# The border of a graph layer and the order of the layer behind it: halved products, an adjacency widened by columns, and one written order

## The chip, the cores and the metric

The kernel runs on one core of a Trainium2 chip. The metric is the device time of one execution in microseconds (us), the median over runs. Five engines matter: TensorE (PE, matrix products and transposes), VectorE (DVE), ScalarE (ACT), GpSimd (POOL) and SyncE (SP, which starts the DMAs). Each of the first four works through its own queue of instructions in order; semaphores make one engine wait for another.

## The reference

Four graph layers run one after another on `x` of shape 16 x 1024 x 64 (batch, node, feature) with one 1024 x 1024 adjacency matrix; each ends in a residual and a normalization over the 64 features:

```python
x = _layernorm(x + _L0_gnn_ref(x, L0_gnn_W, L0_gnn_a, adj), axis=-1)
x = _layernorm(x + _L1_gnn_ref(x, L1_gnn_w0, L1_gnn_b0, L1_gnn_wa, L1_gnn_ba, adj), axis=-1)
x = _layernorm(x + _L2_gnn_ref(x, adj, L2_gnn_W, L2_gnn_a), axis=-1)
x = _layernorm(x + _L3_gnn_ref(x, adj, ...), axis=-1)
```

Layers 0 and 2 are attention with one score per node pair, layer 3 has four heads. Layer 1, which this case is about, has a softmax whose score depends on the neighbour alone, feature by feature:

```python
feat = softplus(x * (INV_SQRT2 * w0) + b0)
scores = feat * wa + ba
attn = softmax(where(adj > 0, scores, -1e9), over the neighbours)
out = einsum('bijd,bjd->bid', attn, feat)
```

So with `E = exp(scores)` layer 1 is `(adj @ (E * feat)) / (adj @ E)`: two products with the plain adjacency, then a quotient.

## The kernel before

The nodes lie in C = 8 chunks of P = 128, the batch in NG = 4 groups of 4 (`xg[g]`), each group in two halves q of two batches.

**Layer 0** (`gat_layer`, lines 900 to 1199) goes batch by batch, t = 0 to 15, with a slot for each of the 8 chunks; tasks of neighbouring batches (evicting, projecting, dividing, residual, statistics, storing) are placed in slots `(t, k)`. Its order is written out by hand: the loop stands under `tc.manual_schedule`, so every engine gets its instructions in program order. The parameter `own` says how many slots behind the last batch belong to that loop; what comes later is returned as the list `ending`.

**Layer 1, preparation** (`prep_l1`, from line 1709) makes, for a group g and half q, nine tasks: `size`, `decay`, `above`, `log` (ACT: the softplus in pieces, 128 x 1024 each), `feature` (DVE adds them), `turn` (PE: 8 transposes of f into the PSUM tile `pf`), `exponents` (DVE finds a maximum over `pf`, ACT makes the exponentials `t`), `back` (PE: 8 transposes of t into the PSUM tile `pe`; ACT rounds that to `hi`, DVE makes `f * pe` and the rest `lo = pe - hi`), and `weighted` (ACT rounds `f * pe` to `hi`, DVE makes its `lo`). So each value is carried as a pair hi + lo in the matmul's rounded type. Group 0 is prepared up to `exponents` within layer 0.

**Layer 1, products** (`product_l1`, line 1829): for each chunk `ic` of 128 nodes, 16 matmuls of 128 x 512 add up into one PSUM tile `po` of the pool `ps_a`, which has two buffers. The stationary operand is a 128 x 128 piece of `aR`, the adjacency in the rounded type; the moving operand holds both halves q, numerator and denominator. `aR` is made from the 16-bit `aT` by eight casts of 128 x 1024 (line 1858), one for each row chunk k, alternately on DVE and ACT, so a product needs all eight.

**Layer 1, quotient** (`average`, line 1840): ACT takes Ln and Exp of the denominators (reciprocal), DVE refines it and multiplies (lines 1846 to 1848, which read `po`), subtracts from x (line 1851) and takes statistics (line 1853, 4 times). At the end of a group `moments`, `root` and `shift` turn these into scale and shift, and `rows` applies them on ACT (line 780, 32 rows of 128 x 64 for a group, four calls of 8).

In layer 1 the loops are not under the hand-written order: the program states tasks in some order, and a planner of the compiler, which knows the engines and the dependencies, decides the order of each engine's queue. In the profile DVE's parts of `average` and of `prep_l1` stand interleaved instruction by instruction.

**The border.** Before the first product of layer 1 stand, in the queues: the eviction of layer 0's last batch (ACT, lines 1022 and 1026), its projection (PE, lines 1043 and 1047), the store of batch 13 (ACT, line 780), the eight casts, the two `back` and the two `weighted` of group 0.

PSUM has room for eight banks: `ps_t` 2, `ps_a` 2, and in layer 0 `ps_g` and `ps_u` with 2 each. In layer 1 `pf` and `pe` use a pool `ps_l` of two tiles of two banks, in the place of `ps_g` and `ps_u`. Layer 2's first steps (`l2_ahead`) run within the last group of layer 1.

Of the kernel before, what the change touches and what calls it, by code (L numbers as in the profile page):

```python
# [8 lines left out]
F32 = mybir.dt.float32  # L9
# [7 lines left out]
P = 128  # L17
# [565 lines left out]
def fast_path(  # L583
# [24 lines left out]
    nc = tc.nc  # L608
    B, N, D = x.shape
    C = N // P  # L610
# [3 lines left out]
    GB = 4  # L614
    NG = B // GB
# [1093 lines left out]
    def prep_l1(g, q):  # L1709
# [36 lines left out]

        def back():
            if q == 0:
                his[g] = l1["halves"].tile([P, C, 2, 2, P], F32R, tag="hi", name=f"hi{g}")
                los[g] = l1["halves"].tile([P, C, 2, 2, P], F32R, tag="lo", name=f"lo{g}")  # L1750
            t = h["t"]
            pe = l1["psum"]("pe")
            for c in range(C):
                nc.tensor.transpose(pe[:, c, :], t[:, c, :], ident)
            hi, lo = his[g][:, :, q, 1, :], los[g][:, :, q, 1, :]
            nc.scalar.copy(hi, pe)
            nc.vector.tensor_tensor(h["f"], h["f"], pe, ALU.mult)
            nc.vector.tensor_tensor(lo, pe, hi.bitcast(F32), ALU.subtract)
# [5 lines left out]

        return [size, decay, above, log, feature, turn, exponents, back, weighted]

# [3 lines left out]
    for task in gat_setup(w_0, "l0", False):  # L1770
        task()
    with tc.tile_pool(name="ps_g", bufs=1, space=bass.MemoryType.PSUM, reuse_waits="tile") as ps_g, tc.tile_pool(
        name="ps_u", bufs=2, space=bass.MemoryType.PSUM, reuse_waits="tile"
# [34 lines left out]
        for q, todo in enumerate(l1_tasks):  # L1808
            t = 7 + 2 * q
            places = (t, 0), (t, 2), (t, 4), (t, 6), (t + 2, 2), (t + 2, 7), (t + 3, 5)  # L1810
            for place, task in zip(places, todo):
                extra.setdefault(place, []).append(task)
        ahead, go = gat_layer(w_0, "l0", False, 5)
        first(ahead)
# [6 lines left out]
    ))  # L1821
    l1_psum = ExitStack()
    ps_l = l1_psum.enter_context(tc.tile_pool(name="ps_l", bufs=2, space=bass.MemoryType.PSUM, reuse_waits="tile"))
    with tc.tile_pool(name="l1", bufs=2, reuse_waits="tile") as pool:
        l1["halves"] = pool
        l1["psum"] = lambda name: ps_l.tile([P, C, P], F32, tag="l", name=name)
        aR = pool.tile([P, C, N], F32R, tag="aR", name="aR", bufs=1)

        def product_l1(g, ic):
            po = ps_a.tile([P, 2, 2, P], F32, tag="acc", name=f"po{g}_{ic}")  # L1830
            for k in range(C):
                for e in (his[g], los[g]):
                    nc.tensor.matmul(  # L1833
                        po.rearrange("p q k f -> p (q k f)"), aR[:, k, ic * P : (ic + 1) * P],
                        e[:, k].rearrange("p q k f -> p (q k f)"),
                        start=(k == 0 and e is his[g]), stop=(k == C - 1 and e is los[g]),
                    )
            return po

        def average(g, ic, po, st):  # L1840
# [13 lines left out]

        ending[0]()
        for i, task in enumerate([l1_tasks[q][-2 + i] for q in range(2) for i in range(2)]):
            for k in range(2 * i, 2 * i + 2):
                (nc.scalar.copy if k % 2 else nc.vector.tensor_copy)(aR[:, k, :], aT[:, k, :])
            task()
        last = ending[1:]  # L1860
        for g in range(NG):
            ahead = [[] for _ in range(C)]
            for q in range(2 if g + 1 < NG else 0):

                for ic, task in zip((q, q, q, q, q + 1, q + 2, q + 2, q + 4, q + 5), prep_l1(g + 1, q)):
                    ahead[ic].append(task)
            if g + 1 == NG:
                for ic, task in zip((1, 2, 3, 3, 4, 5, 6, 6), l2_ahead):
                    ahead[ic].append(task)
            st = pool.tile([P, C * GB, 6], F32, tag="st1", name=f"st{g}")  # L1870
            for ic in range(C):
                po = product_l1(g, ic)
                average(g, ic, po, st)
                for task in ahead[ic] + last[ic : ic + 1]:
                    task()
            y = xg[g].rearrange("p c b d -> p (c b) d")
            mo = {}

            root, finish = moments(st)

            def shift(mo=mo, end=finish):
                mo["n"] = end()

            def rows(c, y=y, mo=mo):
                scaled(y, y, mo["n"], range(c * 8, c * 8 + 8))

            last = [root, shift] + [lambda c=c, rows=rows: rows(c) for c in range(C * GB // 8)]
    l1_pools.close()
# [78 lines left out]
    with tc.tile_pool(name="ps_g", bufs=1, space=bass.MemoryType.PSUM, reuse_waits="tile") as ps_g, tc.tile_pool(  # L1967
        name="ps_p", bufs=1, space=bass.MemoryType.PSUM, reuse_waits="tile"
    ) as ps_p:
        places = [(15, j) for j in (0, 1, 2, 3, 4, 5, 6, 7)]  # L1970
        extra = {p: [task] for p, task in zip(places, ahead)}
        for p, task in zip(((0, 0), (0, 1), (0, 3), (0, 7), (1, 3), (1, 7)), last):
            extra.setdefault(p, []).append(task)

        ending = l2_go(extra)
# [130 lines left out]
```

## Time and profile before

| what | us |
|---|---|
| median of 3 runs | 1978.29 |
| lowest and highest run | 1972.04, 1978.98 |
| profiled execution, its own time | 1970.04 |
| its span, first to last instruction | 1967.8 |
| layer 0 with loading, to its last aggregating matmul | 0 to 279.4 |
| first and last product of layer 1 | 291.4 and 431.0 |
| layer 2's first aggregating matmul | 437.0 |

Over the span PE is busy 96%, DVE 90%, ACT 68%, POOL 4%; the granted PE clock is 0.984 on average. The busy time is an average over stages with different limits, so this document reads the stretch from 280 to 437 us by itself. A line of the timeline gives start, duration, engine, source line, operation, operands and count; in brackets stands the time that the engine sat idle before it and what released it.

### The profile page before, as it was taken

Reading aid. Unit: us, or ns where it says so; the run is one execution under the profiler, and the core shown is the slowest. Engines: PE = TensorE matmul, PEld = TensorE weight load, DVE = VectorE, ACT = ScalarE, POOL = GpSimd, SP = SyncE. Lnnn points to the kernel's source line nnn. Section 1 sums busy time; section 2 is a strip of 40 time slices with the busy share of each in tenths; the row PEclk is TensorE's granted clock in tenths of the full one; section 3 lists DMA queues with packets and bytes.
Section 4 is the critical chain, followed back from the end, with each engine's and each line's share of the span. In section 5 each row is a group of like instructions: output and inputs, shape, how many; then the busy total and the mean of one; then the engine's idle time right before and its main releaser. Section 6 shows DMA issues by size and latency. Waiting matters only on the chain.

```text
span 1967.8 us, 25841 instructions
## 1 busy us (share of the span) xinstructions
PE 1879.4 (96%) x9545; PEld 767.6 (39%) x9545; DVE 1762.7 (90%) x2963; ACT 1332.3 (68%) x2344; POOL 83.0 (4%) x77
## 2 busy tenths in 40 slices
PE   7999989989888899999999999999999999999985
PEld 4444437863333333333333333333333333333332
DVE  5899988879999777798999989999899898998997
ACT  5356567857667776667767767677666776776653
POOL 0000000000000000000000000000000000000001
PEclk8999999999999999999999999999999999999998
DMA  7000000000000120000000000000000100010000
GB/s 179 1 1 1 1 1 1 1 1 1 1 1 3 51 56 12 12 12 19 22 17 12 20 25 12 17 18 22 17 12 18 28 12 17 12 28 17 12 17 18
DMA packets 45748, 35.90 MB, mean 18 GB/s; under 512 B 37295, under 2 KB 37616, under 8 KB 45614
## 3 DMA queue, kind: packets, MB, share of 16 engines
q1 hardware_dynamic: 45310, 34.14, 6.7%
q8 instruction: 77, 1.26, 0.3%
q14 instruction: 57, 0.47, 0.1%
q10 hardware_dynamic: 304, 0.03, 0.0%
HBM read 29.45 MB, written 4.70 MB: 17 GB/s over the span
## 4 chain that ended last, share of the span: by engine, by line
PE 70%; DVE 22%; ACT 5%; issue 1%; DMA 1%; POOL 0%; SPq 0%; DVEq 0%; POOLq 0%; ACTq 0%
PE y L1351 19%; PE s L1336 19%; DVE e L991 7%; PE y_l L1003 6%; PE po L1833 5%; PE y L1516 4%; PE s L1491 4%; DVE e L1344 4%; PE u_l L1015 3%; DVE e L1509 2%; DVE junk L1501 1%; PE phT L1310 1%; ACT e L1340 1%; PE poT L1378 1%; PE ph2T L1452 1%
## 5 line engine op out<-in xcount | busy, mean ns | idle before, releaser
L1340 ACT ACTIVATE e<-s,shift 128x1024 f32<-128x1024 f32 x512 | 539.3, 1123 | 221.2 <-PE s L1336 221.2
L1344 DVE TENSOR_TENSOR e<-e,aT 128x1024 f32<-128x1024 f32 x512 | 596.4, 1215 | 12.9 <-ACT e L1340 12.9
L1336 PE MATMUL s<-hT 64*128 64x512 f32 x2048 | 491.6, 604 | 1.4 <-ACT hT L1319 0.9
L1351 PE MATMUL y<-e,vals 128*64 128x512 f32 x2048 | 485.6, 601 | 5.5 <-DVE e L1344 4.3
L991 DVE SCALAR_TENSOR_TENSOR e<-G_l,q,aT 128x1024 f32<-128x1024 f32 x256 | 315.4, 1275 | 6.4 <-ACT G_l L968 6.3
L1336 PEld LDWEIGHTS s<-hT 64*128 64x128 f32 x2048 | 183.5, 186 | 289.0 <-issue 149.6
L1003 PE MATMUL y_l<-e,vals_l 128*64 128x512 f32 x1024 | 254.2, 616 | 26.9 <-DVE e L991 20.1
L1351 PEld LDWEIGHTS y<-e,vals 128*64 128x64 f32 x2048 | 135.9, 137 | 273.5 <-issue 200.3
L1509 DVE TENSOR_TENSOR e<-e,aT 128x1024 f32<-128x1024 f32 x128 | 156.2, 1225 | 9.8 <-DVE junk L1501 0.5
L1501 DVE SCALAR_TENSOR_TENSOR junk<-e,aN 128x1024 bf16<-128x1024 f32 x120 | 146.1, 1218 | 0.0
L1496 ACT ACTIVATE e<-s,shift 128x1024 f32<-128x1024 f32 x128 | 138.4, 1114 | 0.4 <-PE s L1491 0.4
L1516 PE MATMUL y<-e,h2v 128*64 128x512 f32 x512 | 127.2, 599 | 0.9 <-DVE e L1509 0.9
L1491 PE MATMUL s<-h2T 64*128 64x512 f32 x512 | 125.8, 591 | 0.0
L1003 PEld LDWEIGHTS y_l<-e,vals_l 128*64 128x64 f32 x1024 | 62.3, 138 | 160.4 <-issue 75.7
L1833 PE MATMUL po<-hi,aR 128*128 128x512 f32 x256 | 102.7, 402 | 11.1 <-ACT hi L1762 7.3
L1279 POOL PARTITION_ALL_REDUCE gtop<-top x48 | 55.3, 1152 | 1268.7 <-DVE top L1277 970.0
L1833 PE MATMUL po<-lo,aR 128*128 128x512 f32 x256 | 101.0, 395 | 0.0
L780 ACT ACTIVATE x<-m,bn_shift,bn_rstd 128x64 f32<-128x64 f32 x256 | 88.5, 430 | 0.0
L1491 PEld LDWEIGHTS s<-h2T 64*128 64x128 f32 x512 | 50.0, 186 | 60.2 <-issue 37.3
L1383 ACT COPY zT<-poT 64x512 f32<-64x512 f32 x124 | 72.0, 581 | 1.3 <-PE poT L1378 0.2
L1516 PEld LDWEIGHTS y<-e,h2v 128*64 128x64 f32 x512 | 36.6, 138 | 76.4 <-issue 58.5
L978 ACT ACTIVATE vals_l<-x,p 128x64 f32<-128x64 f32 (+1 forms) x256 | 64.3, 339 | 0.0
(270 smaller groups left out, 1876.1 us busy)
## 6 DMA issues: line engine op xcount, KB each, us to landing
r<-inverse SPq DMA_DIRECT2D x62, 256.0 KB
adj<-in_adj_dram SPq DMA_DIRECT2D x16, 512.0 KB
x<-in_x_dram SPq DMA_DIRECT2D x16, 256.0 KB
out_dram<-res SPq DMA_DIRECT2D x15, 256.0 KB
rows<-yT SPq DMA_DIRECT2D x62, 4.0 KB
sums<-rows SPq DMA_DIRECT2D x31, 8.0 KB
inverse<-rt SPq DMA_DIRECT2D x31, 8.0 KB
out_dram<-res SPq DMA_DIRECT2D x2, 128.0 KB
```

Of the source, the lines that this page charges most:

```text
L991: nc.vector.scalar_tensor_tensor(e, G[b - b % 2][:, b % 2, :], pq[b - b % 2][1][:, k, b % 2 : b % 2 + 1], aT[:, k, :], ALU.max, ALU.mult,)
L1003: nc.tensor.matmul(held["y"][h * D : (h + 1) * D, :], vals[b][:, k, :], e[:, h * HALF : (h + 1) * HALF], start=(k == 0), stop=(k == C - 1),)
L1336: nc.tensor.matmul(s[:, i, :], hT[rows, k * P : (k + 1) * P], hT[rows, cols], start=True, stop=True)
L1340: nc.scalar.activation(e, s, AF.Exp, bias=shifts[b, n])
L1344: nc.vector.tensor_tensor(e, e, bc_mid(aT[:, k, h * HALF : (h + 1) * HALF], 2), ALU.mult)
L1351: nc.tensor.matmul(held[h][i * D : (i + 1) * D, :], vals[b][:, k, :], e[:, i, :], start=(k == 0), stop=(k == C - 1),)
L1491: nc.tensor.matmul(s[:, i, :], hT[rows, (i + k // CH) % 2, k % CH * P : (k % CH + 1) * P], hT[rows, 0, :], start=True, stop=True,)
L1496: nc.scalar.activation(e, s, AF.Exp, bias=shifts[b])
L1501: nc.vector.scalar_tensor_tensor(junk.rearrange("p c q -> p (c q)").bitcast(BF16), e.rearrange("p i q -> p (i q)"), 1.0, aN[:, k, :], ALU. ...
L1509: nc.vector.tensor_tensor(e, e, aT[:, k, :].rearrange("p (i q) -> p i q", i=2), ALU.mult)
L1516: nc.tensor.matmul(held["o"][h * D : (h + 1) * D, :], vals["out", b][:, k, :], e[:, h, :], start=(k == 0), stop=(k == C - 1),)
L1833: nc.tensor.matmul(po.rearrange("p q k f -> p (q k f)"), aR[:, k, ic * P : (ic + 1) * P], e[:, k].rearrange("p q k f -> p (q k f)"), start ...
```

## The change

Five edits, all in layer 1 and its two borders.

1. `back` is cut into `turn_back` (the 8 transposes) and `halves` (the ACT and DVE part). For half 0 of group 0 the transposes move into layer 0's last slots, `(15, 7)`. For this `ps_g` stays open through layer 1; `ps_l` has one tile, and the PSUM tiles of layer 1 come from the two pools in turn (`either`).
2. `aR` is widened by column pairs (`widen(i)`: 128 x 8 x 256, four casts in place of eight): only the first comes before the first product.
3. The first two chunks' products of group 0 are done in halves q: 64 matmuls of 256 columns in place of 32 of 512, all `hi` first, then all `lo`; half 1 is split up while half 0 is being multiplied.
4. `own` goes from 5 to 4: the store of batch 13 leaves the border and comes in chunk 2 of layer 1's first group. `rows` works in eight calls of 4 instead of four of 8.
5. The whole of layer 1 goes under `tc.manual_schedule`: the queues take the written order. In it `average` of a chunk stands behind the next chunk's product (`late`), and the preparation of the next group has its chunks: half 0 in 0,0,1,1,2,2,3,3,4,5 and half 1 in 2,2,3,3,4,4,5,5,6,7, in the order of the ten tasks.

```diff
@@ prep_l1
-        def back():
+        def turn_back():
+            h["pe"] = l1["psum"]("pe")
+            for c in range(C):
+                nc.tensor.transpose(h["pe"][:, c, :], h["t"][:, c, :], ident)
+
+        def halves():
...
-            t = h["t"]
-            pe = l1["psum"]("pe")
-            for c in range(C):
-                nc.tensor.transpose(pe[:, c, :], t[:, c, :], ident)
+            pe = h["pe"]
@@ layer 0
+        extra.setdefault((B - 1, 7), []).append(l1_tasks[0][7])
-        ahead, go = gat_layer(w_0, "l0", False, 5)
+        ahead, go = gat_layer(w_0, "l0", False, 4)
@@ layer 1
+        def product_l1(g, ic, po=None, q=None):
+            po = po or ps_a.tile([P, 2, 2, P], F32, tag="acc", name=f"po{g}_{ic}")
+            part = slice(0, 2) if q is None else slice(q, q + 1)
+            order = [(k, e) for k in range(C) for e in (his[g], los[g])]
+            if q is not None:
+                order = [(k, e) for e in (his[g], los[g]) for k in range(C)]
...
+        def widen(i, copy):
+            cols = slice(i * 2 * P, (i + 1) * 2 * P)
+            copy(aR[:, :, cols], aT[:, :, cols])
...
-        ending[0]()
-        for i, task in enumerate([l1_tasks[q][-2 + i] for q in range(2) for i in range(2)]):
-            for k in range(2 * i, 2 * i + 2):
-                (nc.scalar.copy if k % 2 else nc.vector.tensor_copy)(aR[:, k, :], aT[:, k, :])
-            task()
-        last = ending[1:]
+        stored, projected, *last = ending
+        last.insert(2, stored)
+        def opening():
+            (pe_0, halves_0, weighted_0), (pe_1, halves_1, weighted_1) = (l1_tasks[q][7:] for q in range(2))
+            projected()
+            widen(0, nc.vector.tensor_copy)
+            pe_1()
+            halves_0()
+            weighted_0()
+            pos = [product_l1(0, ic, q=0) for ic in range(2)]
+            halves_1()
+            weighted_1()
+            for ic, po in enumerate(pos):
+                product_l1(0, ic, po, 1)
+            widen(1, nc.scalar.copy)
+            widen(2, nc.vector.tensor_copy)
+            widen(3, nc.scalar.copy)
+            return pos
...
-                for ic, task in zip((q, q, q, q, q + 1, q + 2, q + 2, q + 4, q + 5), prep_l1(g + 1, q)):
-                    ahead[ic].append(task)
+                    for q, ics in enumerate(((0, 0, 1, 1, 2, 2, 3, 3, 4, 5), (2, 2, 3, 3, 4, 4, 5, 5, 6, 7))):
+                        for ic, task in zip(ics, prep_l1(g + 1, q)):
+                            ahead[ic].append(task)
...
+                ends = last_of[g - 1]
+                for task, ic in zip(ends, (0, 1, 1, 2, 4, 5, 6, 6, 7, 7) if g else range(C)):
                     ahead[ic].append(task)
...
-            for ic in range(C):
-                po = product_l1(g, ic)
-                average(g, ic, po, st)
-                for task in ahead[ic] + last[ic : ic + 1]:
-                    task()
+                for ic in range(C):
+                    po = before.pop(0) if before else product_l1(g, ic)
+                    if late:
+                        late()
+                    late = lambda g=g, ic=ic, po=po, st=st: average(g, ic, po, st)
+                    for task in ahead[ic]:
+                        task()
+                late()
...
-                scaled(y, y, mo["n"], range(c * 8, c * 8 + 8))
+                    scaled(y, y, mo["n"], range(c * 4, c * 4 + 4))
...
+        with tc.manual_schedule(engines=in_order):
+            last = groups()
```

## The prediction

> **What bounds the kernel now.** First I read the page: PE is busy 96% of the span and DVE 90%, so the time is decided stage by stage. Then I read the stretches of layer 1 (columns: stretch, its length, busy us and instructions of PE, PEld, DVE, ACT, POOL, the granted PE clock, DMA share, GB/s).
>
> ```profile
> 282.00:292.00 10.00, 2.71 (x22) 2.30 (x20) 7.61 (x10) 10.00 (x13) 0.00 (x0) 0.73 0.00 0
> 292.00:310.00 18.00, 17.96 (x76) 14.37 (x75) 14.18 (x51) 13.48 (x26) 0.00 (x0) 0.87 0.00 0
> 350.00:370.00 20.00, 18.20 (x90) 15.10 (x89) 18.09 (x41) 17.59 (x29) 0.00 (x0) 1.00 0.00 1
> 370.00:390.00 20.00, 20.00 (x104) 16.82 (x103) 15.94 (x56) 17.95 (x47) 0.00 (x0) 1.00 0.00 1
> ```
>
> At the border PE works 2.7 of 10 us while ACT is full. Behind it PE is full, but DVE and ACT stand at 80 to 90%: little room on any of the three. Next, PE's timeline (start, us, engine, line, operation; in brackets the idle time before it and what ended it):
>
> ```profile
> 281.10 1.11 PE L1047 MATMUL po<-l_wd,yT_l 64*128 64x64 f32 x16
> 282.13 1.97 PE L1754 MATMUL pe<-ident,t 128*128 128x128 f32 x16
> 291.39 1.22 PE L1833 MATMUL po<-hi,aR 128*128 128x512 f32 x2 [7.29 <-ACT hi L1762]
> ...
> 296.23 0.63 PE L1833 MATMUL po<-lo,aR 128*128 128x512 f32 x1
> 296.65 0.48 PE L1833 MATMUL po<-hi,aR 128*128 128x512 f32 x1
> ...
> 297.44 0.39 PE L1833 MATMUL po<-lo,aR 128*128 128x512 f32 x1
> ...
> 330.26 0.47 PE L1833 MATMUL po<-hi,aR 128*128 128x512 f32 x1 [1.81 <-DVE top L1742]
> ...
> 361.30 0.47 PE L1833 MATMUL po<-hi,aR 128*128 128x512 f32 x1 [1.80 <-DVE t L1848]
> ```
>
> From 291.4 to 296.7 the matmuls follow each other by 0.43 us, then by 0.228: the slow clock after the wait costs some 14 x 0.2 = 2.8 us. Up to the last product's end at 431.0 PE otherwise waits only 0.2 + 1.81 + 1.80. So layer 1 is 139.6 us from its first product, of which 139.6 - 3.8 - 2.8 = 133.0 is work at full clock. By rows: 512 x 0.228 = 116.7, 104 transposes x 0.112 = 11.6, layer 2's pieces (1.7 + 2.1); together 132.1. Third, ACT at the border:
>
> ```profile
> 279.96 2.76 ACT L780 ACTIVATE x<-m,bn_shift,bn_rstd 128x64 f32<-128x64 f32 x8
> 282.62 1.04 ACT L1858 CAST aR<-aT 128x1024 fp32r<-128x1024 bf16 x1
> 283.56 1.00 ACT L1756 CAST hi<-pe 128x1024 fp32r<-128x1024 f32 x1
> ```
>
> The store of batch 13 and four casts keep it from the four roundings. Last, one `average` on DVE, and the prices of the preparation (groups by line: count, busy us, mean ns, idle):
>
> ```profile
> 420.07 0.42 DVE L1846 TENSOR_TENSOR t<-po,r 128x256 f32<-128x256 f32 x1 [1.13 <-ACT r L1844]
> 420.53 0.43 DVE L1847 SCALAR_TENSOR_TENSOR r<-t,r 128x256 f32<-128x256 f32 x1
> 420.99 0.42 DVE L1848 TENSOR_TENSOR t<-po,r 128x256 f32<-128x256 f32 x1
> 421.45 0.42 DVE L1851 TENSOR_TENSOR x<-x,t 128x256 f32<-128x256 f32 x1
> 421.91 0.60 DVE L1853 BATCH_NORM_STATS2 st<-x 128x6 f32<-128x64 f32 x4
> ```
>
> ```profile
> L1741 DVE TENSOR_SCALAR_CACHE_REDUCE t<-pf,wa 128x1024 f32<-128x1024 f32 x6 | 7.7, 1284 | 4.0 <-PE pf L1735 4.0
> L1730 DVE TENSOR_TENSOR f<-f,t 128x1024 f32<-128x1024 f32 x6 | 7.3, 1222 | 2.5 <-ACT t L1727 2.5
> L1745 ACT ACTIVATE t<-pf,down,wa 128x1024 f32<-128x1024 f32 x6 | 7.2, 1200 | 5.0 <-DVE bn_shift L771 2.8 <-DVE down L1744 2.2
> ```
>
> An `average` holds DVE for 4 x 0.46 + 0.52 = 2.36. Ln and Exp take 0.88 until DVE can begin. DVE's other 1024-column passes (`feature`, `f * pe`, both `lo`) follow each other by 1.13, and another engine has their result after 1.26. The maximum with its two small steps takes 1.78; ACT's exponential 1.25 to the result, 1.11 to ACT's next.
>
> **The change part by part: the border.** The 8 moved transposes (0.89) enter layer 0's tail, where PE has no gap from 265.8 to 279.4: the last `u` ends at 280.3. The eviction ends 280.95 (0.6), projecting 283.0 (0.98 + 1.04), the other 8 transposes 283.9. Beside that, ACT rounds the first `hi` at 281.0, no longer behind the store. DVE widens the first columns 280.3 to 281.6 (two of its casts, 2 x 0.63) and makes `f * pe` until 282.85; ACT's second rounding is done at 283.9. So the first product starts at 283.9, not 291.4, at full clock, since PE was idle 0.7 only. It waits 0.3 for `lo`, and the halves end at 291.6.
>
> Two operations there have no row. A 256-column matmul costs between the 0.112 of a 128-column transpose and the 0.228 of 512 columns; I take 0.114, the half. The upper end would cost 64 x 0.114 = 7.3, of which the wait named next hides 4.5. A cast of 2048 columns by pairs is between two casts on DVE (1.25) and two passes of L1763's kind (2.3): 0 to 1 us at the start; I take the casts.
>
> **The new wait.** The third product needs a `po` buffer, and there are two. It waits for the first `average`, whose Ln stands on ACT behind, in order: last rounding (to 287.3), two widenings (2 x 1.9, to 291.1), `size` and `decay` of group 1 (2.1), the exponential of layer 0's last batch (0.6). Ln starts at 293.8, DVE is done with `po` at 294.7 + 3 x 0.46 = 296.1. PE waits 4.5.
>
> **The written order of layer 1.** Before, the planner let DVE slip the preparation between the steps of an `average`. The listing of the changed queues shows the plain order: PE has product 2, the 8 `pf`, product 3, the 8 `pe`, product 4, `pf`, product 5, `pe`, products 6 and 7. Each transpose block waits for a chain through ACT and DVE, and the product queued behind it, with its Ln and `average`, waits too. A product is 3.66, a block 0.89. Five waits in a group that prepares the next:
>
> (a) `pf` of half 0, group 1. ACT begins product 0's Ln 0.8 after that product (the group's `moments` and `root` stand before it). Then 0.88, `average` 2.36, four shift steps 0.88, 4 rows 1.32, 0.88, `average` 2.36, `feature` 1.26: together 9.94, against two products, 7.32. Wait 3.4. In group 0 the chain starts with the third product: rest of the first `average` 0.98, residual 1.44, 2.36, 1.26, together 6.04 against 3.66: 2.4.
>
> (b) `pe` of half 0. From `pf`: 0.66 until Ln and Exp are there (4 rows before them), 2.36, 1.78, 1.25, together 6.05, against 0.89 + 3.66: 1.5 (1.8 in group 0, which stores batch 13 there).
>
> (c) `pf` of half 1. From the start of half 0's exponential: ACT 1.11 + `above` 1.13 + `log` 0.95, then Ln and Exp 0.88; DVE `average` 2.36, `f * pe` 1.13, `lo` 1.13, `feature` 1.26: 9.95, against 1.25 + 0.89 + 3.66 = 5.80. Wait 4.15 in every group.
>
> (d) `pe` of half 1. From `feature`: 2.36 + 1.13 + 1.78 + 1.25 = 6.5, less 0.1 of overlap, against 0.04 + 4.55: 1.8.
>
> (e) The next group's product 0. From the second exponential's start: ACT 1.11 + 4 rows 1.32 + 0.84, DVE 2.36 + 1.13 + 1.13 + 2.36 + 1.26: 11.5, against 1.25 + 0.89 + 7.32 = 9.46: 2.1; in group 0, with less on ACT, 1.0.
>
> Group 0: 2.4 + 1.8 + 4.15 + 1.8 + 1.0 = 11.2. Groups 1 and 2: 3.4 + 1.5 + 4.15 + 1.8 + 2.1 = 13.0 each. Group 3 prepares nothing. Together 37.2.
>
> **Clock.** After 7.3 us of idling the slow clock cost 2.8; after 4.96 us (before layer 2's first matmuls, 437.0) sixteen took 5.35 in place of 3.65, so 1.7; after 1.8 us nothing. The waits of 3.4 to 4.5 (six) lie between. Each is followed by a wait of 1.5 to 2.4 that takes up most of it, since its chain does not go through the slowed product: 0 to 6 together, I take 1.
>
> [...]
>
> **Nothing for the rest.** Layer 2 begins behind the same chain as before (Ln, `average`, moments, first e: 431.0 to 437.0). Its first 16 `rows` on ACT are as many before the eviction at 448.1, which waits 1.8 for PE; without that cover one call of 4 is 1.3. No DMA and no POOL instruction moves.
>
> **Sum.** 283.9 + 0.3 + 133.0 + 4.5 + 37.2 = 458.9, against 431.0: +27.9, with the clock +29. The profiled execution took 1970.04 (span 1967.8); it would become 1999. The three runs lie at 1972.04 to 1978.98, mean 1976.4, so I forecast 1976.4 + 29 = 2005.
>
> **Rivals.**
> (1) Faster: the border decides, and the chains hide under the products as they do now. For it: before, PE waits 3.8 us with the same total of DVE work (about 16 to 18 of 20 us). Against it: that was reached by interleaving. Place: wait (c). If DVE could put `feature` and `turn` ahead of `average` there, and likewise elsewhere, 37.2 would go: 458.9 - 37.2 = 421.7, or -9, some 1967. It decides if the five waits stay under (431.0 - 421.7) / 3 = 3 us a group.
> (2) Half of the waits: chains shorter than my rows, 6 us a group. +9, some 1986.
> (3) The slow clock stays: each of the six long waits costs 2.8, uncovered, and so does the opening's upper end (+2.8). 29 - 1 + 17 + 3 = 48, some 2024; half of it, 2015.
> (4) The written order is not kept in the queues, or costs nothing either way: the listing speaks against it.
>
> **How the numbers follow.** My forecast 77%, (3) 12%, (2) 6%, (1) 4%, (4) 1%. The range: low end, the lowest run plus 22 (chains 0.5 shorter at each of 15 waits), 1994; high end 2018, the highest run plus 29 and half of (3). That leaves out (1), (2), (4) and a part of (3), some 16%. A measurement of this kernel can tell about 0.5% (10 us): faster 0.04, same 0.03, slower 0.93.
>
> **What would show it.** Right: the first product near 284 at full clock; a PE wait of 4 to 5 us before the third product on DVE's L1848 step; in the groups 0 to 2 PE idle before `pf` on `feature` and before `pe` on the exponential, the second `pf` the longest; granted clock under 1.0 somewhere between 296 and 420; last product near 459; layers 2 and 3 as long as before. Wrong: PE waits under 10 us in all behind the third product, or a layer 3 of another length.

## The result and the profile after

The changed kernel takes 2002.48 us (median, 2000.28 to 2004.13) beside 1978.63 us of the kernel before (1972.04 to 1979.49), so the medians differ by 23.9; the ratio on record is 1.0143, with a 95% interval of 1.0119 to 1.0168, that is +23.5 to +33.2 us. The forecast was 2005, by +29.

The profiled execution took 2003.76 us (span 2001.4), 33.7 more than that of before. Three pieces make that up. Layer 0's last aggregating matmuls (tile `u_l`, below: the last `u`) end at 285.34 in place of 279.40 (+5.9). From there to the end of layer 1's last product it is 178.49 us in place of 151.76 (+26.7). From the last product to the end of the span it is 1537.6 in place of 1536.6 (+1.0). The first piece is mostly not the change: the experiments below with the old border, whose instructions up to `u` are those of before, have that end at 281.8 and 283.8. So it moves by some 4 us from execution to execution, and 0.9 is the eight transposes moved in front of it; in the nine traces with the new border it lies between 281.0 and 285.3.

The same view of stretches as before (stretch, length, busy us and instructions of PE, PEld, DVE, ACT, POOL, then the granted PE clock, DMA share, GB/s), for the border, the start of group 0, and three stretches of about a group's length in groups 1, 2 and 3:

```profile
286.00:296.00 10.00, 9.78 (x85) 9.26 (x86) 9.62 (x12) 7.27 (x6) 0.00 (x0) 1.00 0.00 0
296.00:314.00 18.00, 12.14 (x56) 9.50 (x55) 12.63 (x46) 13.69 (x24) 0.00 (x0) 0.91 0.01 2
...
333.00:379.00 46.00, 36.49 (x166) 29.21 (x166) 32.22 (x93) 32.07 (x67) 0.00 (x0) 0.96 0.00 1
379.00:424.00 45.00, 36.08 (x160) 29.16 (x159) 31.56 (x92) 31.11 (x64) 0.00 (x0) 0.92 0.00 1
424.00:458.00 34.00, 32.25 (x155) 26.26 (x153) 21.92 (x77) 18.59 (x53) 0.35 (x1) 1.00 0.00 0
```

The border is now full on PE and DVE. Behind it nothing is: in the two stretches of groups 1 and 2 PE is busy 79 to 80%, and DVE and ACT only 69 to 70%, where before they stood at 80 to 90%. All three engines became idler at once, so none of them is the bound; the timelines below show that they wait for each other. The last stretch, where no group is prepared, has PE full again.

PE's timeline of the changed kernel, the lines with waits (start, us, line, operation; in brackets the idle time before it and what ended it):

```profile
289.30 1.21 PE L1848 MATMUL po<-hi,aR 128*128 128x256 f32 x8
...
301.32 0.47 PE L1848 MATMUL po<-hi,aR 128*128 128x512 f32 x1 [3.80 <-DVE t L1867]
...
302.80 0.63 PE L1848 MATMUL po<-hi,aR 128*128 128x512 f32 x1
303.23 0.63 PE L1848 MATMUL po<-lo,aR 128*128 128x512 f32 x1
...
307.12 1.09 PE L1735 MATMUL pf<-ident,f 128*128 128x128 f32 x8 [0.30 <-DVE f L1730]
...
313.63 1.09 PE L1750 MATMUL pe<-ident,t 128*128 128x128 f32 x8 [1.77 <-ACT t L1745]
...
322.39 1.15 PE L1735 MATMUL pf<-ident,f 128*128 128x128 f32 x8 [3.99 <-DVE f L1730]
```

```profile
352.41 1.09 PE L1735 MATMUL pf<-ident,f 128*128 128x128 f32 x8 [3.51 <-DVE f L1730]
...
358.44 1.09 PE L1750 MATMUL pe<-ident,t 128*128 128x128 f32 x8 [1.30 <-ACT t L1745]
...
367.20 1.57 PE L1735 MATMUL pf<-ident,f 128*128 128x128 f32 x8 [4.02 <-DVE f L1730]
...
383.74 0.50 PE L1848 MATMUL po<-lo,aR 128*128 128x512 f32 x1 [1.62 <-DVE lo L1765]
...
412.68 1.94 PE L1735 MATMUL pf<-ident,f 128*128 128x128 f32 x8 [3.89 <-DVE f L1730]
```

The first product starts 3.96 us after the last `u` (before 11.99), the third waits 3.80 for the first `average`, and then each group stops at the same places: the two `pf` blocks, the first `pe` block, the next group's first `lo`. PE's waits between the first and the last product add up to 29.9 us (before 3.8). Another 11.6 us are left: first to last product is 174.53, less the waits, less the 133.0 of work at full clock. Most of that is the slow clock (the lines of 0.63 us at 302.80, spaced by 0.43 in place of 0.228). The trace has PE at half clock for 17.1 us of this stretch, in five pieces of 3.41, so the clock cost at most 8.5. The other 3 us or more are small losses at full clock, such as these: the half-width matmuls take 64 x 0.12 = 7.7 in place of 32 x 0.228 = 7.3, and the two matmuls that begin behind a wait start 0.31 apart (301.32 and 301.63) in place of 0.228. One group lasts 45.5 us from its first `pf` to the next group's.

Which chain that is, is seen on the other two engines in group 2. DVE and ACT there:

```profile
409.06 1.21 DVE L1759 TENSOR_TENSOR f<-f,pe 128x1024 f32<-128x1024 f32 x1
410.18 1.22 DVE L1760 TENSOR_TENSOR lo<-pe,hi 128x1024 fp32r<-128x1024 f32 x1
411.31 1.22 DVE L1730 TENSOR_TENSOR f<-f,t 128x1024 f32<-128x1024 f32 x1
412.44 0.42 DVE L1865 TENSOR_TENSOR t<-po,r 128x256 f32<-128x256 f32 x1
...
414.80 1.21 DVE L1765 TENSOR_TENSOR lo<-f,hi 128x1024 fp32r<-128x1024 f32 x1
415.92 1.28 DVE L1741 TENSOR_SCALAR_CACHE_REDUCE t<-pf,wa 128x1024 f32<-128x1024 f32 x1
```

```profile
410.30 1.05 ACT L1764 CAST hi<-f 128x1024 fp32r<-128x1024 f32 x1 [0.64 <-DVE f L1759]
417.69 1.21 ACT L1745 ACTIVATE t<-pf,down,wa 128x1024 f32<-128x1024 f32 x1 [6.35 <-DVE down L1744]
```

DVE is busy without a gap, in the written order: `f * pe`, `lo`, and only then `feature`, for which PE waits 3.9 us (its `pf` starts at 412.68). Then it does a whole `average` and the other `lo` ahead of the maximum, for which ACT waits 6.35 us. Elsewhere DVE waits in its turn, for ACT's Exp ahead of an `average`; the sums of both are shown with e9_fine below.

### The profile page after: what moved, and what is told of

The parts are those of the page before. It is cut to its first block, busy times and chain, and to the rows that moved or that the text cites. A ratio compares the mean times of both kernels' runs of the same rounds, so it can differ in the third digit from the quotient of the medians.

```text
span 2001.4 us, 25894 instructions
## 1 busy us (share of the span) xinstructions
PE 1892.1 (95%) x9577; PEld 776.0 (39%) x9577; DVE 1767.5 (88%) x2961; ACT 1338.1 (67%) x2342; POOL 83.1 (4%) x77
## 4 chain that ended last, share of the span: by engine, by line
PE 64%; DVE 27%; ACT 6%; issue 2%; DMA 1%; POOL 0%; SPq 0%; DVEq 0%; POOLq 0%; ACTq 0%
PE y L1351 18%; PE s L1336 17%; DVE e L991 7%; PE y_l L1003 6%; DVE e L1344 5%; PE y L1516 4%; PE s L1491 4%; PE u_l L1015 3%; DVE e L1509 2%; PE po L1848 2%; DVE junk L1501 2%; ACT e L1340 1%; ACT x L780 1%; PE ph2T L1452 1%; PE phT L1310 1%
## 5 line engine op out<-in xcount | busy, mean ns | idle before, releaser
L1848 PE MATMUL po<-hi,aR 128*128 128x512 f32 (+1 forms) x272 | 103.6, 398 | 4.0 <-DVE t L1867 3.8
L1848 PE MATMUL po<-lo,aR 128*128 128x512 f32 (+1 forms) x272 | 101.9, 391 | 4.0 <-DVE lo L1765 3.9
```

The costliest lines, as they stand in the source:

```text
L1848: nc.tensor.matmul(po[:, part].rearrange("p q k f -> p (q k f)"), aR[:, k, ic * P : (ic + 1) * P], e[:, k, part].rearrange("p q k f -> p ( ...
```

## The experiments

My theory (W) was the forecast's: the places in the written order cost the time, on the chains through ACT and DVE. A stricter form (W2) says that such a wait has no price of its own: the chain held in order sets the length of a group, and a wait that is taken away at one place comes back at a later one. Rivals: the border's pieces cost (B), the slow clock does (C), PE's own work does (P). H names what halving the first products gains.

In the table, times are from each run's one profile; "waits" are PE's between the first and last product, "rest" is what is left of first to last after 133.0 of work and the waits (of e3 also less its 11.0 of extra work), "half clock" is the time between the first and last product for which the trace granted PE half its clock (half of that is the most it can have cost), and the period is from the first `pf` of group 2's preparation to that of group 3's, where there is one order.

| run | ratio to before | u to first product | u to last | waits | rest | half clock | period |
|---|---|---|---|---|---|---|---|
| before | 1 | 11.99 | 151.76 | 3.8 | 3.0 | 5.5 | |
| changed | 1.0143 | 3.96 | 178.49 | 29.9 | 11.6 | 17.1 | 45.5 |
| e1_planned | 1.0003 | 6.50 | 152.23 | 6.9 | 5.9 | 4.2 | |
| e2_written_only | 1.0173 | 12.14 | 188.18 | 26.0 | 17.1 | 33.8 | 45.7 |
| e3_dummy | 1.0136 | 3.96 | 178.52 | 22.9 | 7.7 | 10.2 | 45.4 |
| e4_feature_early | 1.0154 | 3.96 | 182.53 | 29.9 | 15.7 | 33.8 | 46.6 |
| e5_open_first | 1.0137 | 3.96 | 180.39 | 27.3 | 16.2 | 30.7 | 45.7 |
| e6_rewritten | 1.0045 | 3.96 | 164.12 | 16.3 | 10.9 | 16.7 | 38.1 |
| e7_border_avg | 1.0000 | 10.12 | 152.84 | 4.6 | 5.1 | 6.2 | |
| e8_whole | 1.0143 | 8.17 | 180.21 | 24.0 | 15.1 | 28.6 | 45.4 |
| e9_fine | 0.9978 | 3.96 | 148.99 | 6.5 | 5.5 | 6.5 | 33.8 |
| e10_fine_old_border | 1.0005 | 12.16 | 156.12 | 6.4 | 4.6 | 6.6 | 33.8 |

### The order alone and the border alone

```diff
-        with tc.manual_schedule(engines=in_order):
+        if True:
             last = groups()
```

> The changed kernel with one edit undone: layer 1 stands no longer under the written order, the planner orders the queues; the whole border edit stays. Theory W (the written order costs the time): the 37 us of the five waits a group go, up to a few us that the planner leaves (before: 3.8), and the border's gain of about 7 us stays, less a wait before the third product of 3 to 4. So 30 to 33 us under the changed kernel, about 1970 to 1974, and 3 to 8 us (0.2 to 0.4%) under the kernel before. Rival B (halves, column casts, the two PSUM pools or the earlier transposes cost it): it stays within 10 us of the changed kernel, 1990 or more. Rival C (the slow clock): follows W here, as the waits that cause it go.

1973.76 us beside 1973.97, ratio 1.0003 (0.9990 to 1.0017). All pieces of the border stay, and the whole loss is gone: it was the order, not the pieces, and B falls. But the border's gain is gone too, where 3 to 8 us under the kernel before were expected. ACT's timeline of this run shows where:

```profile
280.83 2.75 ACT L780 ACTIVATE x<-m,bn_shift,bn_rstd 128x64 f32<-128x64 f32 x8
283.49 0.56 ACT L1022 COPY yT_l<-y_l 128x512 f32<-128x512 f32 x1
283.95 0.57 ACT L1026 COPY ysum_l<-u_l 128x512 f32<-128x512 f32 x1
...
285.66 1.90 ACT L1857 CAST aR<-aT 128x2048 fp32r<-128x2048 bf16 x1
```

The planner puts the store of batch 13 ahead of the eviction again, and a widening between the roundings, so the first product comes 6.5 us after `u`. What is left of the gain, 5.5 us, is given back behind it: the waits are 6.9 in place of 3.8 (the longest, 2.93, stands before the third product) and the rest 5.9 in place of 3.0. The slow clock is not it, with 4.2 us at half clock against 5.5 before.

```diff
-        extra.setdefault((B - 1, 7), []).append(l1_tasks[0][7])
-        ahead, go = gat_layer(w_0, "l0", False, 4)
+        ahead, go = gat_layer(w_0, "l0", False, 5)
...
-            widen(0, nc.vector.tensor_copy)
-            pe_1()
...
+            tasks = [lambda: (pe_0(), halves_0()), weighted_0, lambda: (pe_1(), halves_1()), weighted_1]
+            for i, task in enumerate(tasks):
+                for k in range(2 * i, 2 * i + 2):
+                    (nc.scalar.copy if k % 2 else nc.vector.tensor_copy)(aR[:, k, :], aT[:, k, :])
+                task()
+            return []
```

> The written order alone: the border as before (eight casts by rows, transposes and roundings of both halves behind them, whole products, the store of batch 13 in the border), and layer 1 under the written order with the new places. Theory W: all five waits a group stay, 30 to 37 us, and nothing is won at the border; the wait before the third product goes, as no casts are left behind the roundings. So the changed kernel plus 4 to 8 us, 2006 to 2011, against before 27 to 33 us slower. Rival B: near the kernel before, within 10 us of 1978.

2009.88 us, ratio 1.0173 (1.0147 to 1.0200): the written order behind the border of before is as slow as the changed kernel and slower. Groups last the same 45.7 us. The interval overlaps that of the changed kernel; the trace has the last product 9.7 us later after `u`, of which 8.2 is the later start. Against before it is some 34 us by the ratio, a little over the 27 to 33 expected. So with one order in both, the new border is worth something, some 6 us by the ratios and 10 by the traces.

### Is it the slow clock or the work of PE?

```diff
             h["pf"] = l1["psum"]("pf")
+            if q == 1 and g >= 1: l1["idle"](g - 1)
...
+        def idle(g):
+            pt = ps_t.tile([P, HALF], F32, tag="t", name=f"idle{g}")
+            for i in range(16): nc.tensor.matmul(pt, aR[:, i // 2, :P], his[g][:, i // 2].rearrange("p q k f -> p (q k f)"), start=i == 0, stop=i == 15)
```

> The changed kernel with 16 more matmuls of 128x512 (3.66 us by rows of the products) ahead of the second transposes of f in chunk 4 of each of the groups 0 to 2, into an unused PSUM bank; nothing reads them. Theory W: there PE waits 4.0 us for a chain through ACT and DVE that does not pass PE, so the 11 us of added PE work are covered: within 2 us of the changed kernel, 2001 to 2005, and PE's idle time before those transposes falls from 4 us to under 0.7 each. Rival P (PE's own work bounds the layer): 11 us more, about 2013. Rival C (the slow clock costs the time): the added work keeps the clock up, so the kernel gets 3 or more us faster.

```profile
317.01 3.79 PE L1896 MATMUL idle<-hi,aR 128*128 128x512 f32 x16
321.16 1.07 PE L1736 MATMUL pf<-ident,f 128*128 128x128 f32 x8 [0.37 <-DVE f L1730]
...
327.44 1.09 PE L1751 MATMUL pe<-ident,t 128*128 128x128 f32 x8 [1.54 <-ACT t L1746]
```

Eleven microseconds of extra matmuls cost nothing: 2001.44 us, ratio 1.0136, u to last 178.52 against 178.49. The three waits they fill go from 3.99, 4.02 and 3.89 to 0.37, 0.36 and 0.24, and the `pf` block lands where it landed. The clock behind them is full (behind the block at 321.16 the matmuls of 512 columns are 0.22 to 0.24 apart once the first two have started), but that gains nothing either: the `pe` block, which follows a slow product in the changed kernel and waits 0 to 0.2, now waits 1.54. Here the slow clock only fills what would be the next wait. The table says the same: in the changed kernel, e2, e3, e5 and e8 the time at half clock goes from 10.2 to 33.8 us, and the period stays at 45.4 to 45.7. C and P fall.

### Does a wait have a price of its own?

One number changed: `feature` of the second half goes from chunk 4 to chunk 3, ahead of the `average` and the two passes that delay it.

```diff
-                    for q, ics in enumerate(((0, 0, 1, 1, 2, 2, 3, 3, 4, 5), (2, 2, 3, 3, 4, 4, 5, 5, 6, 7))):
+                    for q, ics in enumerate(((0, 0, 1, 1, 2, 2, 3, 3, 4, 5), (2, 2, 3, 3, 3, 4, 5, 5, 6, 7))):
```

> The changed kernel with one place changed: feature of half 1 in chunk 3, not 4, so DVE adds the softplus before the average of chunk 3 and the two passes of half 0. Theory W as the prediction has it, with each wait priced by itself: wait (c), 4 us in each of three groups, goes, 12 us less, about 1990. Theory W2 (the group's length is set by DVE and ACT, each held in order by Ln, Exp and the averages; a wait removed on PE comes back at the next transposes): wait (c) goes, but the wait before the pe transposes of half 1 grows from 0 to 2 by 3 to 4 us and one of about 1 us stands before a product: within 2 us of the changed kernel.

```profile
318.53 0.47 PE L1848 MATMUL po<-hi,aR 128*128 128x512 f32 x1 [1.07 <-DVE t L1867]
...
328.15 1.97 PE L1750 MATMUL pe<-ident,t 128*128 128x128 f32 x8 [5.72 <-ACT t L1745]
```

The longest wait is gone, and the kernel is not faster: 2005.45 us, ratio 1.0154. The second `pe` block, which hardly waited, now waits 5.72, 3.96 and 4.99 in the three groups, more than the 3 to 4 expected. So the wait came back with something on top: u to last is 4.0 us longer than in the changed kernel, outside the 2 us that W2 gave, and on the side away from W. The opening gives the same answer, with the first average ahead of the last widening:

```diff
             widen(2, nc.vector.tensor_copy)
+            average(0, 0, pos[0], st)
             widen(3, nc.scalar.copy)
```

> The changed kernel with one move: the first chunk's average stands ahead of the last widening in the opening, so Ln no longer waits behind 1.9 us of cast, size, decay and the exponential of layer 0's last batch. The wait before the third product (3.8 us) falls to about 0.6. Theory W2 (the chain through ACT and DVE sets the time): the later tasks of ACT come as much later, so the first transposes of f in chunk 2 wait for feature 4 to 6 us in place of 0.3 to 2.4: within 2 us of the changed kernel from layer 0's last matmul to layer 1's last product (178.5 us there). Theory W with each wait priced by itself: 3.2 us less.

```profile
296.50 0.47 PE L1848 MATMUL po<-hi,aR 128*128 128x512 f32 x1 [0.48 <-DVE t L1867]
...
305.97 1.97 PE L1735 MATMUL pf<-ident,f 128*128 128x128 f32 x8 [5.58 <-DVE f L1730]
```

The third product waits 0.48 in place of 3.80, and the `pf` block behind it 5.58 in place of 0.30; 2003.00 us, ratio 1.0137, and u to last is 1.9 us longer. In both runs a wait that was removed came back at the place that W2 names, and nothing was gained. A third form of the same question undoes the halving:

```diff
-            pos = [product_l1(0, ic, q=0) for ic in range(2)]
+            pos = []
             halves_1()
             weighted_1()
-            for ic, po in enumerate(pos):
-                product_l1(0, ic, po, 1)
+            pos = [product_l1(0, ic) for ic in range(2)]
```

> The changed kernel without the halving: the first two chunks' products whole, behind the second half's splitting. Theory W2: the third product waits for the first average, whose Ln stands on ACT behind the widenings, size and decay; that place does not depend on the halving. So the products begin about 4 us later, the wait before the third falls from 3.8 to under 0.5, and all behind it is unmoved: within 1.5 us of the changed kernel (178.5 us from layer 0's last matmul to layer 1's last product). Rival H (the halving brings its 3.7 us of earlier product work): 3 to 4 us slower.

The first product starts 4.2 us later, the third no longer waits, and the last ends 1.7 us later after `u`, a little over the 1.5 expected; 2002.55 us, ratio 1.0143 (1.0127 to 1.0160). So in the changed kernel the halving's earlier start of 4.2 us is worth 1.7 by one trace of each and nothing by the medians, since what it gains is waited for at the third product.

### Can a written order do without it?

First other places for whole tasks, the preparation set partly ahead of an `average` (with the opening's `average` as in e5, and two of the ends of a group at other chunks, not shown):

```diff
-                    for q, ics in enumerate(((0, 0, 1, 1, 2, 2, 3, 3, 4, 5), (2, 2, 3, 3, 4, 4, 5, 5, 6, 7))):
+                    for q, ics in enumerate(((-1, -1, -1, -1, -2, -2, -3, 2, -5, 6), (1, 1, 1, 1, -3, 2, 3, -5, -7, 6))):
                         for ic, task in zip(ics, prep_l1(g + 1, q)):
-                            ahead[ic].append(task)
+                            (ahead[ic] if ic > 0 else soon_l1[-ic - 1]).append(task)
...
+                    for task in soon_l1[ic]: task()
+                    if late: late()
```

> Layer 1 still under the written order, with other places: the softplus passes of both halves in chunks 1 and 2, each transposes block one chunk or more behind what feeds it, the exponentials and the two passes of a half ahead of the average of their chunk, and the opening's average as in the run before. If W2 holds, it is the places and not the writing by hand that cost the time. By the same sums of rows the waits on PE are about 20 us in place of 42: 18 to 24 us less than the changed kernel, about 1980, still 5 to 9 us over the kernel before, since the steps of an average stay together. Rival (a written order as such is slow, whatever its places): within 5 us of the changed kernel, 1998 or more.

1983.68 us (about 1980 expected), ratio 1.0045 (1.0029 to 1.0061), and 38.1 us a group: places alone, with the same instructions, give back some 19 us of the 28. Then a mixed form, the opening written and the groups left to the planner:

```diff
-        with tc.manual_schedule(engines=in_order):
-            last = groups()
+        first_two, st_0 = [], pool.tile([P, C * GB, 6], F32, tag="st1", name="st0")
+        with tc.manual_schedule(engines=in_order): first_two += opening()
+        last = groups()
...
```

> The opening alone under the written order (with the first average ahead of the last widening), the groups behind it left to the planner, average right behind its product. Theory: the border's gain is real but was given back in the planned kernel because the planner put a store of 8 rows and group 1's softplus into the border and left a wait of 2.9 us before the third product. With the border written out, the first product comes 4 us after layer 0's last matmul, and the wait before the third product is about 2: 144 to 148 us from layer 0's last matmul to layer 1's last product, against 151.8 before and 152.2 in the planned kernel. 4 to 7 us (0.2 to 0.35%) faster than before. Rival (the border's gain is always given back within the first group, as DVE and ACT stand full there): no difference, within 2 us.

```profile
283.43 1.67 PE L1043 MATMUL po<-l_ind,ysum_l 128*128 128x2 f32 x8 [2.38 <-ACT ysum_l L1026]
...
291.16 2.07 PE L1848 MATMUL po<-hi,aR 128*128 128x256 f32 x8 [2.27 <-ACT hi L1764]
```

1974.33 us, ratio 1.0000 (0.9989 to 1.0012). The early start I expected did not come: the planner laid store rows and group 1's softplus between the written instructions, and the first product came 10.1 us after `u`. The run says nothing on what an early start is worth.

Last, one written order in which the tasks themselves are cut: `average` into Ln and Exp (A), three DVE steps (B), subtraction and statistics (C); `halves` and `weighted` into single instructions. P is a product, p and q the two halves' steps by number (0 to 4 the softplus, 5 `turn`, 6 `exponents`, 7 `turn_back`, 8 to 12 the roundings, `f * pe` and rests), M the moments and E the ends of the group before, whose last chunk is -1:

```diff
+        ORDER = (
+            "P0 A-1 B-1 C-1 M0 p0 A0 E0 B0 p1 P1 p2 E1 C0 p3 p4 A1 q0 P2 B1 q2 q1 C1 p5 q3 A2 p6 P3 E2 q4 A3 q5 "
+            "B2 p7 p8 E3 C2 q6 P4 E4 q7 A4 B3 p9 C3 P5 q9 p11 q11 B4 p10 q8 E5 C4 A5 q10 P6 B5 P7 q12 p12 E6 C5 "
+            "E7 A6 E8 B6 C6 E9 "
+        )
...
```

> Border written as changed, and layer 1 still in one written order, but in a finer one: average is cut into three pieces (Ln and Exp; three DVE steps; the subtraction with the statistics), halves and weighted into their single instructions, and these are laid between each other, with the first average's Ln and Exp ahead of the last widening. Theory W2 (the places in the written order cost, not that it is written, and not the border's pieces): no chain is held up any more. By durations from the trace of before the last product would end some 147 us after layer 0's last u if the clock stayed full; with 3 to 5 us for the slow clock, 150 to 152 (changed kernel 178.5, before 151.8); PE waits inside layer 1 under 6 us; ratio to before 0.997 to 1.001. Rival W' (a written order costs as such, since no one order suits what the engines do at run time): PE waits of 12 us or more, ratio 1.005 or more.

1970.81 us beside 1973.90, ratio 0.9978 (0.9964 to 0.9992): faster than both kernels, by 4.3 us (1.6 to 7.1) than before (3.1 by the medians alone). Groups last 33.8 us, where 8 products and 4 blocks alone are 8 x 3.66 + 4 x 0.89 = 32.8. PE waits are 6.5, a little over the 6 expected, and the last product comes 1 us earlier than the 150 expected. The gain against before is shown by the twelve executions: the one with the profile was the slowest of them, and in it the 2.8 us won up to the last product are lost again behind it (1539.5 to the end of the span, before 1536.6). The stretch of group 1, which had 36.49, 32.22 and 32.07 us of PE, DVE and ACT in the changed kernel, is full again:

```profile
333.00:379.00 46.00, 45.43 (x219) 37.34 (x218) 42.23 (x129) 41.84 (x80) 0.00 (x0) 1.00 0.00 1
```

The waits around the preparation, over 300 to 424 us (groups: count, busy us, mean ns, idle before and what ended it), first of the changed kernel, then of this one, which gets through more averages in the same 124 us (28 against 22):

```profile
L1865 DVE TENSOR_TENSOR t<-po,r 128x256 f32<-128x256 f32 x22 | 9.3, 423 | 32.8 <-ACT r L1863 31.6 <-PE pf L1735 1.2
...
L1735 PE MATMUL pf<-ident,f 128*128 128x128 f32 x48 | 8.4, 332 | 18.9 <-DVE f L1730 18.9
...
L1745 ACT ACTIVATE t<-pf,down,wa 128x1024 f32<-128x1024 f32 x6 | 7.3, 1209 | 31.5 <-DVE down L1744 21.0 <-DVE ln_step L712 6.3 <-PE po L1848 4.2
```

```profile
L1869 DVE TENSOR_TENSOR t<-po,r 128x256 f32<-128x256 f32 x28 | 11.7, 418 | 8.4 <-ACT r L1864 8.2
...
L1745 ACT ACTIVATE t<-pf,down,wa 128x1024 f32<-128x1024 f32 x6 | 7.2, 1198 | 1.1 <-DVE down L1744 1.1
L1735 PE MATMUL pf<-ident,f 128*128 128x128 f32 x48 | 6.5, 281 | 2.4 <-DVE f L1730 2.4
```

PE's 18.9 us of waiting before `pf` became 2.4, ACT's 31.5 before the exponentials 1.1, and DVE's 32.8 before an `average` 8.4, by the same instructions in another order. A written order as such does not cost; where its instructions stand does. How much of the last 13 us from e6 to here came from cutting the tasks and how much from new places, no run tells apart. The same order behind the old border:

```diff
-            widen(0, nc.vector.tensor_copy)
+            for i, tasks in enumerate(((pe_0, *rest_0[:3]), rest_0[3:], (pe_1, *rest_1[:3]), rest_1[3:])):
+                for k in range(2 * i, 2 * i + 2):
+                    (nc.scalar.copy if k % 2 else nc.vector.tensor_copy)(aR[:, k, :], aT[:, k, :])
...
```

> The same finer written order behind the border as before: eight casts by rows, the store of batch 13 ahead, no transposes moved, whole products. Theory H2 (the earlier start is kept where nothing waits behind it): first product 12 us after the last u, last product 4 to 7 us later than in the run with the changed border beside it, a ratio higher by 0.002 to 0.0035. Rival (what the border gains is given back within the first group, as with the planner's order): last product within 2 us of that run, ratio within 0.001 of it.

1975.50 us beside the same 1973.90, ratio 1.0005 (0.9991 to 1.0020). The new border is worth 4.7 us by the medians, 7.1 by the traces (u to last 156.12 against 148.99, 4 to 7 expected). The two intervals just touch, so that its size is loose; that it is kept behind both written orders (e2 and here) and lost under the planner's is what the traces show.

## Why the prediction was right

**The border.** Right in its mechanism: the first product starts 3.96 us after the last `u` (forecast 3.6) at full clock (granted 1.00 from 286 to 296). The two operations without a row were priced well: the 256-column matmuls follow each other by 0.12 us (taken 0.114, upper bound 0.228), a widening takes DVE 1.23 and ACT 1.85 (taken 1.25 and 1.9). The halves end 12.2 us after `u` (11.3), and the third product starts at 16.0 (15.8): the chain for the first `average` was sized within 0.2 us, and the wait is 3.8 in place of 4.5 because the products ahead of it took longer.

**The waits of the written order.** The places are those named. Wait (c), the second `pf`, is 3.99, 4.02 and 3.89 (4.15); (a) in groups 1 and 2 is 3.51 and 3.18 (3.4); (b) is 1.77, 1.30 and 0 (1.8, 1.5, 1.5); (e) is 0.68, 1.62 and 1.65 (1.0, 2.1, 2.1). Too large were (d), 0, 0 and 0.23 in place of 1.8, and (a) in group 0, 0.30 in place of 2.4.

**The clock.** The forecast let the waits stand at full length and took 1 us, 0 to 6 allowed, for what the slow clock costs beyond them. In the run the half clock lasted 17.1 us and cost at most 8.5. With the small losses 11.6 us came on top of the work, and the waits were shorter by as much: 3.8 + 26.1 in place of 4.5 + 37.2. Waits and rest together are 41.5; the forecast had 4.5 + 37.2 + 1 = 42.7 (first product to last: 174.53 against 175.0, or 176.0 with the clock's 1). So the split was off by some 11 us each way, and the sum held. That this is the mechanism named, a slow product taken up by the wait behind it, is shown for (d): with the clock full in e3 it is 1.54 to 1.57, near the 1.8 forecast, in place of 0 to 0.23. For (a) of group 0, behind the slow third product, and for the rest of the difference it is argued, and how close the sum came is partly luck.

Behind the waits of 3.99 and 4.02 half the clock followed, but the wait of 3.51 at 352.41 left it full, and one of 2.40 in e9_fine was followed by matmuls at 0.43 us. The last section sets two of the changed kernel's waits side by side.

**What the working did not see.** Adding the waits gave a right sum and would have been a wrong guide for mending: (c), priced at 4.15 in each group, was worth nothing when it was removed alone (e4), as was the third product's (e5). A wait that is taken away comes back at a later place, and a sum of separate waits cannot show that.

**The rivals.** Rival (1), hidden chains, put the last product 141.4 us after `u` (421.7 - 280.3). The changed kernel is not that case, but e9_fine comes to 148.99, 2.8 under before: its waits and rest are 12.0 together, where the rival kept 4.8 (0.3 + 4.5), and that difference of 7.2 is nearly all that is missing. Rival (2) did not come about. (3) was too high twice: its 17 us (2.8 for each of six waits) stand against five pieces of half clock of at most 1.7 each, 8.5 together, and "uncovered" failed with e3. (4) does not stand: the waits lie where the listing had them.

**Nothing for the rest** holds: 5.84 us from the last product to layer 2's first `y_l` (5.83), and 1.0 us over the rest of the kernel.

## What to carry to other kernels

In a written order over several engines, look for the loop that no engine's busy share shows: when PE, DVE and ACT all become idler at once, as here, look whether each is waiting for another's place in its queue. Do not price such waits one by one; compare the length of a whole period with the work of its fullest engine (45.5 against 32.8 here), and cut and interleave the tasks until the two meet. A gain at a border can be taken back by a wait behind it: the halving's 4.2 us became 1.7 (e8), and the planner's earlier start of 5.5 us came to nothing (e1). Set the same order behind both borders to see what is left.

## What the runs showed that was not expected

Waits of the same size have both outcomes for the clock (3.51 none; 3.18 and 2.40 slow), so a single wait's length does not tell. In the trace of the changed kernel the half clock begins five times within layer 1, at 302.76, 323.24, 367.61, 398.33 and 411.99, and each time it lasts 3.41 us; within it matmuls of 512 columns are spaced by 0.43 in place of 0.228. Stretches of that length at two waits, the one of 3.80 that ends at 301.32 and the one of 3.51 that ends at 352.41 (stretch, length, busy us and instructions of PE, PEld, DVE, ACT, POOL, the granted PE clock, DMA share, GB/s):

```profile
299.35:302.76 3.41, 1.44 (x6) 1.24 (x7) 2.79 (x9) 3.35 (x6) 0.00 (x0) 1.00 0.00 0
302.76:306.17 3.41, 3.41 (x9) 2.63 (x8) 3.24 (x11) 3.38 (x7) 0.00 (x0) 0.50 0.02 5
...
350.55:353.96 3.41, 1.55 (x11) 1.46 (x12) 2.62 (x8) 2.45 (x7) 0.00 (x0) 1.00 0.00 0
353.96:357.37 3.41, 3.19 (x15) 2.29 (x13) 2.96 (x10) 0.18 (x1) 0.00 (x0) 1.00 0.00 0
```

The wait of 3.80 left 1.44 us of PE work in the 3.41 us ahead of 302.76, and half the clock followed; ahead of the other four beginnings PE was busy 0.85, 0.41, 0.45 and 0.21 us in as long a stretch. The wait of 3.51 lies partly in 347.13 to 350.55, with 1.77 us of PE work, and partly in 350.55 to 353.96, with 1.55, and the clock stayed full. This depends on where a stretch is taken to begin: over the wait itself, 348.90 to 352.41, PE was busy 0.01 us, and the clock stayed full too. It was read from one trace and tested by no run, so what sets the clock is not shown. Nor does PE's work just ahead tell elsewhere: in the kernel before PE was busy throughout from 546.02 to 549.43, and the clock granted from there to 552.84 was 0.50; and the same opening began at the full clock in the changed kernel (1.21 us for the first eight matmuls) and at the slow one in e9_fine (2.07).

Extra matmuls in a wait that others set cost nothing (u to last 178.52 in e3_dummy, 178.49 in the changed kernel), and the clock behind them stayed full: from 333 to 379 no two successive matmuls of 512 columns in e3_dummy are spaced by 0.43, where the changed kernel has some (from 369.00) and was granted 0.96.

Where the planner has the work around a region with a written order, it lays other instructions between those of the region: in e7_border_avg the early start of 3.96 us became 10.12.
